# Attention and trigonometric FFN on one core: square roots as jobs of pairs of tiles, with new orders

## The chip, the cores and the metric

The kernel runs on 1 core of one Trainium2 chip. The time is device microseconds of one execution, as the median of several runs. The engines are TensorE (PE; PEld is its weight load), VectorE (DVE), ScalarE (ACT), GpSimd (POOL) and SyncE (SP), which issues nearly all DMAs.

## The reference, cut to what matters

`x` is (2, 2048, 512) float32, 4096 rows of 512. Context `ctx` is (2, 77, 512) with a mask over the 77 keys.

```python
def xattn(q, kv, mask):          # hid = 512, one head
    Q, K, V = q @ Wq + bq, kv @ Wk + bk, kv @ Wv + bv
    s = where(mask, einsum('bqh,bkh->bqk', Q, K) / sqrt(512), -1e9)
    return softmax(s) @ V @ Wo + bo

def ffn(x):
    real = x @ cos(theta + theta_noise)
    imag = x @ sin(phi + phi_noise)
    return sqrt(real * real + imag * imag)

x = x + xattn(layernorm(x), ctx, mask)
x = x + ffn(layernorm(x))
```

## The kernel before, in words

The rows are 32 tiles of 128 (t = 0 to 31). Two tiles are a pair (k2 = t // 2, 16 of them; one load of 512 KB each), four tiles a block (k = t // 4, 8 of them; softmax goes by block). First the weights are prepared: `Wq` and `Wk` are folded with the context into a 77-column matrix (scores), `Wv` and `Wo` into `VO`, and cos and sin of theta and phi into f16 weights, high part `WH` and low part `WL`.

Each tile then passes through: layernorm (statistics L612 to L630, normalised `xna` L638 or L640), split into an f16 high part (L643) and low part (L647), a transpose by DMA (L651, `xTa`), scores on TensorE (L694, L697, `s`), row maximum (L705), exp (L714, `e`), split of the probabilities into f16 parts in the buffer `E` (high L724 or L726, low L730 and L731; job names `eh`, `el`), a transpose of a whole block's `E` by DMA (L755, `et`, one for each block, `et7` the last), the product with `VO` (L794, L798, `o`; o28 is the one of tile 28), division and residual (L803), the second layernorm (`mw` L809, `xnb` or `xq` L861 on VectorE, L863 on ScalarE; the sum of squares L844 on ScalarE or L839 to L841 on VectorE; `vr` L849, L850), again a split (L643, L647 or, for the fast pairs, L872 to L884) and a transpose (`xTb` L651, `xU` L890; the job is `Tb`).

Then the FFN. Ordinary tiles take two groups of products into `f` (L945; f12 is that of tile 12) and square it on ScalarE (L998). Pairs 9 to 14 are "fast": both tiles share products of combined operands (L916, banks `f0`, `f1`, `fb`), a copy out of a bank (L926) and additions of banks on VectorE (L930, "combines") before the square (L933). Last, for every tile: the sum of the two squares (`ma`, L1004, into `mg`), the square root with the second layernorm's scale (`rt`, L1008, on ScalarE, table "sqrt"), the addition to `x` (`ou`, L1012) and the store (`st`, L1015). `ma` and `ou` may be on VectorE or POOL. Two tiles share a buffer `mg`. Tile 31 goes in three parts of 256, 128 and 128 columns.

None of this is in program order. Every step is an entry of `Jobs` with its engine, its assumed duration, the jobs it depends on, and the buffers it takes and releases. `Jobs.order()` is a planner: it goes through the jobs by a due time that stands for each job in the table `KEY`, charges `TABLE` = 1.28 us where a ScalarE job needs another table (`tab`), and writes out one order for every engine's queue, SP's included. The table `ENGINE` says for which jobs the second choice of engine is taken. The kernel is then issued in that order; on the chip each engine takes its queue strictly in order.

In the kernel before, the roots are one job for a block, which asks for four sums `ma` and both `vr`:

```python
add(("rt", k), "ACT", 2.58, [("ma", u, 0) for u in g] + [("vr", u // 2) for u in g if u % 2], lambda g=g: roots(g), tab="sqrt")
for u in g:
    add(("ou", u, 0), "POOL", 1.3, [("rt", k)], ...)
    add(("st", u, 0), "SP", 0.45, [("ou", u, 0)], ...)
```

The last block has a root for each tile, and for each part of tile 31.

Of the kernel before, what the change touches and what calls it, by code (L numbers as in the profile page):

```python
# [18 lines left out]
D = 512  # L19
# [16 lines left out]
ENGINE = {('VT', 1): 'DVE', ('wqT', 2): 'DVE', ('wqT', 3): 'DVE', ('tr', 1, 0, 2): 'DVE', ('tr', 1, 0, 3): 'POOL', ('tr', 1, 1, 2): 'DVE', ('tr', 1, 1, 3): 'POOL', ('xna', 0): 'DVE', ('loa', 4): 'POOL', ('loa', 5): 'POOL', ('loa', 6): 'POOL', ('loa', 7): 'POOL', ('loa', 8): 'POOL', ('loa', 9): 'POOL', ('hia', 10): 'DVE', ('loa', 10): 'POOL', ('nm1', 5): 'POOL', ('hia', 11): 'DVE', ('loa', 11): 'POOL', ('hia', 12): 'DVE', ('nm1', 6): 'POOL', ('loa', 13): 'POOL', ('loa', 14): 'POOL', ('xna', 17): 'DVE', ('loa', 21): 'POOL', ('xna', 23): 'DVE', ('hia', 23): 'DVE', ('loa', 25): 'POOL', ('xna', 26): 'DVE', ('hia', 26): 'DVE', ('loa', 26): 'POOL', ('loa', 27): 'POOL', ('xna', 30): 'DVE', ('loa', 30): 'POOL', ('loa', 31): 'POOL', ('et', 0, 1): 'ACT', ('et', 0, 2): 'ACT', ('eh', 3, 0): 'ACT', ('eh', 6, 0): 'ACT', ('eh', 7, 0): 'ACT', ('xnb', 0): 'ACT', ('xnb', 1): 'ACT', ('hib', 3): 'DVE', ('s2', 2): 'POOL', ('hib', 4): 'DVE', ('lob', 4): 'POOL', ('xnb', 5): 'ACT', ('hib', 5): 'DVE', ('xnb', 6): 'ACT', ('xnb', 7): 'ACT', ('hib', 7): 'DVE', ('lob', 8): 'POOL', ('xnb', 9): 'ACT', ('lob', 9): 'POOL', ('s2', 5): 'POOL', ('xnb', 10): 'ACT', ('lob', 10): 'POOL', ('bn2', 11): 'DVE', ('lob', 11): 'POOL', ('xnb', 12): 'ACT', ('hib', 12): 'DVE', ('lob', 13): 'POOL', ('s2', 7): 'POOL', ('xnb', 14): 'ACT', ('s2', 8): 'POOL', ('xnb', 16): 'ACT', ('hib', 16): 'DVE', ('xnb', 17): 'ACT', ('hib', 18): 'DVE', ('lob', 19, 1): 'POOL', ('s2', 10): 'POOL', ('xnb', 20): 'ACT', ('xnb', 21): 'ACT', ('qs', 20, 0): 'POOL', ('qs', 20, 2): 'POOL', ('lob', 21, 0): 'POOL', ('xnb', 22): 'ACT', ('xnb', 23): 'ACT', ('qs', 22, 1): 'POOL', ('qs', 22, 2): 'POOL', ('lob', 22, 0): 'POOL', ('lob', 22, 1): 'POOL', ('lob', 23, 0): 'POOL', ('xnb', 24): 'ACT', ('xnb', 25): 'ACT', ('qs', 24, 2): 'POOL', ('lob', 25, 0): 'POOL', ('lob', 25, 1): 'POOL', ('s2', 13): 'POOL', ('xnb', 26): 'ACT', ('xnb', 27): 'ACT', ('qs', 26, 1): 'POOL', ('qs', 26, 2): 'POOL', ('hib', 26): 'DVE', ('lob', 26, 0): 'POOL', ('lob', 26, 1): 'POOL', ('lob', 27, 0): 'POOL', ('lob', 27, 1): 'POOL', ('xnb', 28): 'ACT', ('xnb', 29): 'ACT', ('qs', 28, 0): 'POOL', ('hib', 28): 'DVE', ('hib', 29): 'DVE', ('lob', 29, 1): 'POOL', ('s2', 15): 'POOL', ('xnb', 30): 'ACT', ('lob', 30): 'POOL', ('xnb', 31): 'ACT', ('lob', 31): 'POOL', ('ma', 0, 0): 'DVE', ('ma', 3, 0): 'DVE', ('ou', 0, 0): 'DVE', ('ma', 4, 0): 'DVE', ('ma', 5, 0): 'DVE', ('ma', 7, 0): 'DVE', ('ou', 4, 0): 'DVE', ('ou', 5, 0): 'DVE', ('ou', 6, 0): 'DVE', ('ou', 7, 0): 'DVE', ('ma', 8, 0): 'DVE', ('ma', 9, 0): 'DVE', ('ou', 9, 0): 'DVE', ('ou', 10, 0): 'DVE', ('ma', 12, 0): 'DVE', ('ma', 15, 0): 'DVE', ('ou', 13, 0): 'DVE', ('ma', 16, 0): 'DVE', ('ma', 17, 0): 'DVE', ('ma', 18, 0): 'DVE', ('ou', 16, 0): 'DVE', ('ou', 17, 0): 'DVE', ('ou', 18, 0): 'DVE', ('ou', 23, 0): 'DVE', ('ma', 26, 0): 'DVE', ('ou', 24, 0): 'DVE', ('ou', 25, 0): 'DVE', ('ou', 26, 0): 'DVE', ('ou', 27, 0): 'DVE', ('ma', 28, 0): 'DVE', ('ma', 29, 0): 'DVE', ('ma', 30, 0): 'DVE', ('ma', 31, 0): 'DVE', ('ma', 31, 384): 'DVE'}  # L36
# [4 lines left out]
class Jobs:  # L41
# [11 lines left out]
    def add(self, name, eng, dur, deps, fn, alloc=(), rel=(), tab=None, size=0.0, alts=(), after=None, bank=None, lag=0.0, port=False, lead=0.87, alone=None):  # L53
        assert name not in self.jobs, name
        opts = [(eng, dur, port)] + [(a[0], a[1], len(a) > 3 and a[3]) for a in alts]
        for a in alts:
            if ENGINE.get(name) == a[0]:
                eng, dur, fn, port = a[0], a[1], a[2], len(a) > 3 and a[3]
        self.jobs[name] = dict(
            eng=eng, dur=dur, deps=list(deps), fn=fn, alloc=[t if isinstance(t, tuple) else (t, name) for t in alloc], rel=rel, tab=tab,  # L60
            size=size, opts=opts, after=after, bank=bank, lag=lag, port=port, lead=lead, alone=1.55 * size if alone is None else alone,
        )
# [117 lines left out]
def xattn_trig_ffn(  # L180
# [20 lines left out]
    V, A, G, T, S = nc.vector, nc.scalar, nc.gpsimd, nc.tensor, nc.sync  # L201
# [4 lines left out]
    NBLK = NT // 4  # L206
# [4 lines left out]
    wk = ctx.enter_context(tc.tile_pool(name="work", bufs=2))  # L211
# [7 lines left out]
    add = jobs.add  # L219
# [16 lines left out]
    warm = cst("warm", [P, 512], F16)  # L236
# [9 lines left out]
    R = cst("R", [P, 2, NB, D], F16)  # L246
# [6 lines left out]
    cg = cst("cg", [P, NB * NK])  # L253
    cgd = cst("cgd", [P, NB * NK])
    gs = cst("gs", [P, 1])
    bcol = cst("bcol", [P, 4, NC])
    brow = cst("brow", [16, P])
    msk = cst("msk", [P, NB, NK], mask.dtype)
    keep = cst("keep", [P, NB * NK])
    kscale = cst("kscale", [P, NB * NK])  # L260
    kneg = cst("kneg", [P, NB * NK])
    cxT = cst("cxT", [P, NC, NB * NK])
    VT = cst("VT", [P, NC, NB * NK])
    KT = cst("KT", [P, NC, NB * NK])
# [90 lines left out]
    for hc in range(NC):  # L355
# [5 lines left out]
            alts=(("DVE", 0.29, lambda hc=hc: V.tensor_scalar(VT[:, hc], D_["vt", hc], bcol[:, 2, hc : hc + 1], None, ALU.add)),))  # L361
# [41 lines left out]
    ssm, e2m, scm = bound("m", 1, ["mks"], P)  # L403
    ssv, _, scv = bound("v", NB, [f"vos{b}" for b in range(NB)], P, False)
    sce = cst("sce", [P, 1])
# [53 lines left out]
    for b in range(NB):  # L459
# [3 lines left out]
            alts=(("DVE", 0.6, lambda b=b: vo_ev(b, V.tensor_copy)),))  # L463
        sumsq(f"vos{b}", lambda b=b: vot(b), ssv[:, b : b + 1], 0.42, [("vb", b)])
        add(("vh", b), "ACT", 0.62, [("voe", b), "scv"], lambda b=b: vo_h(b, A),
            alts=(("DVE", 0.34, lambda b=b: vo_h(b, V), True),))
# [17 lines left out]
    for dc in range(NC):  # L484
# [4 lines left out]
            alts=(("DVE", 0.6, lambda ev=ev: ev(V.tensor_copy)),))  # L489
        add(("mk", dc), "PE", 1.05, [("wqT", dc)] + KTs + ([("mk", dc - 1)] if dc else []), lambda dc=dc: mk_mm(dc),  # L490
            alloc=("f",) if dc % 2 == 0 else (), rel=(("wqTh", dc // 2),))
    for h in range(2):
        def ev(E, h=h):
# [5 lines left out]
            alts=(("DVE", 0.45, lambda ev=ev: ev(V.tensor_copy)),))  # L499
# [4 lines left out]
        alts=(("DVE", 0.4, lambda: V.tensor_scalar(Mk[:, :, 0], D_["M"], scm, None, ALU.mult), True),))  # L504
# [93 lines left out]
    for i, a, b, op in SUMS if FAST else ():  # L598
        add(("ts", i), "DVE", 1.13, [quarter[a], quarter[b]] + before[i], lambda i=i, a=a, b=b, op=op: tsum(i, a, b, op, V), port=True,
            rel=(a, b), alts=(("POOL", 2.3, lambda i=i, a=a, b=b, op=op: tsum(i, a, b, op, G), True),))  # L600
# [67 lines left out]
    for t in range(NT):  # L668
        k = t // 2
# [7 lines left out]
        if t < 4 * DIRECT:  # L677
            add(("pa", t), "PE", 0.44, [("xna", t)], lambda t=t: turn("a", t), alloc=("m",), rel=(("xna", t),))
            add(("Ta", t), "ACT", 0.48, [("pa", t)], lambda t=t: keep_t(t, A.copy), alloc=("xTa",), rel=(("pa", t),),
                alts=(("DVE", 0.6, lambda t=t: keep_t(t, V.tensor_copy)),))  # L680
# [3 lines left out]
            alts=(("POOL", 1.17, lambda t=t: lo("a", t, G), True),))  # L684
# [321 lines left out]
    def root(t, w):  # L1006
        m = D_["mg", t // 2][:, t % 2, w[0] : w[1]]
        A.activation(m, m, AF.Sqrt, scale=VR[t // 2][:, t % 2 : t % 2 + 1])  # L1008

    def outp(t, E, w):  # L1010
        xo = xb[t][:, w[0] : w[1]]
        E.tensor_tensor(xo, xo, D_["mg", t // 2][:, t % 2, w[0] : w[1]], ALU.add)  # L1012

    def store(t, w):
        S.dma_start(of[t][:, w[0] : w[1]], xb[t][:, w[0] : w[1]])  # L1015

    for t in range(NT):
        k = t // 4
# [51 lines left out]
        if t % 4 == 3 and not last:  # L1070
            def roots(g):
                for t in g:
                    root(t, (0, D))
            g = range(t - 3, t + 1)
            add(("rt", k), "ACT", 2.58, [("ma", u, 0) for u in g] + [("vr", u // 2) for u in g if u % 2], lambda g=g: roots(g), tab="sqrt")
            for u in g:
                add(("ou", u, 0), "POOL", 1.3, [("rt", k)], lambda u=u: outp(u, G, (0, D)), rel=(("ma", u - u % 2, 0),),
                    alts=(("DVE", 0.6, lambda u=u: outp(u, V, (0, D)), True),), port=True)
                add(("st", u, 0), "SP", 0.45, [("ou", u, 0)], lambda u=u: store(u, (0, D)), rel=(("x", u // 2),), size=0.73, alone=0.87)
        elif k == NBLK - 1:  # L1080
            for w in parts:
                f = (w[1] - w[0]) / D
                q = (t, w[0])
                add(("rt",) + q, "ACT", 0.27 + 0.45 * f, [("ma",) + q, ("vr", t // 2)], lambda t=t, w=w: root(t, w), tab="sqrt")
                add(("ou",) + q, en, (0.6 if E is V else 1.3) * f, [("rt",) + q], lambda t=t, E=E, w=w: outp(t, E, w), port=True, rel=(("ma", t - t % 2, 0),))
                add(("st",) + q, "SP", 0.45, [("ou",) + q], lambda t=t, w=w: store(t, w), rel=(("x", t // 2),), size=0.73 * f, alone=0.87 * f)
# [37 lines left out]
```

## Time and profile before

| | us |
|---|---|
| median of 3 runs (lowest, highest) | 236.86 (236.34, 236.89) |
| the profiled execution: time | 237.07 |
| its span | 235.2 |
| PE, PEld busy | 225.7, 124.8 |
| DVE, ACT, POOL busy | 206.7, 193.7, 116.4 |

The mean granted clock of TensorE is 0.998. Busy time is the sum of an engine's instructions in the span; time and span differ by 1.87 us of start and end that the trace does not cover. All positions in the text are microseconds from the start of the span. `<-` in a row separates what an instruction writes from what it reads, or, behind an idle time, names what ended it.

### The profile page before, as it was taken

The page shows a single profiled execution, that of the slowest core. Times are in us where ns is not written, and L with a number is a line of the kernel's source. Part 1 is how long each engine was busy: PE and PEld are TensorE (multiplying, and loading weights), DVE is VectorE, ACT ScalarE, POOL GpSimd, SP SyncE. Part 2 cuts the span into 40 slices and gives each one's busy share as a digit, 9 for nine tenths or more (in the row PEclk, how much of TensorE's full clock was granted, in tenths as well). Part 3 has the DMA queues.
Part 4 walks back from the last instruction along what each step waited for, and adds up shares of the span by engine and source line. Part 5 has one row for each costly group of instructions (what it writes and reads, how often), then busy time and mean ns, then how long its engine had stood idle before and what let it go on. Part 6 is the DMA issues. An engine that isn't in the chain of part 4 may idle for free. (4 is left out here: it accounts for less than half of the span.)

```text
span 235.2 us, 4452 instructions
## 1 busy us (share of the span) xinstructions
PE 225.7 (96%) x1438; PEld 124.8 (53%) x1438; DVE 206.7 (88%) x592; ACT 193.7 (82%) x372; POOL 116.4 (49%) x116
## 2 busy tenths in 40 slices
PE   7999899999999999999999999999999898999992
PEld 2698797655445454444454456444444443444472
DVE  1779998899999999877977989999999979998972
ACT  2077999999999998997789499997879993897853
POOL 5116493931570706521762670631983589277340
PEclk9999999999999999999999999999999999999999
DMA  3999999955879799299879998998495746485543
GB/s 106 385 387 386 387 277 227 342 115 102 166 94 184 194 193 245 49 258 252 139 136 249 221 197 135 188 307 155 92 156 117 197 117 121 80 164 171 145 169 134
DMA packets 92725, 45.51 MB, mean 193 GB/s; under 512 B 79681, under 2 KB 80389, under 8 KB 92703
## 3 DMA queue, kind: packets, MB, share of 16 engines
q1 hardware_dynamic: 92431, 45.21, 81.6%
q8 instruction: 11, 0.18, 0.3%
q14 instruction: 11, 0.09, 0.1%
q10 hardware_dynamic: 144, 0.02, 0.0%
q0 software_dynamic: 128, 0.01, 0.0%
HBM read 17.12 MB, written 8.39 MB: 108 GB/s over the span
## 5 line engine op out<-in xcount | busy, mean ns | idle before, releaser
L945 PE MATMUL f<-WH,xTb 128*128 128x512 f16 (+2 forms) x352 | 87.0, 360 | 0.0
L945 PEld LDWEIGHTS <-xTb 128*128 128x128 f16 x528 | 49.1, 98 | 52.5 <-DMA xTb<-xsb 0.5
L945 PE MATMUL f<-WL,xTb 128*128 128x512 f16 (+2 forms) x176 | 50.2, 360 | 0.0
L916 PEld LDWEIGHTS <-xU 128*128 128x128 f16 x252 | 24.5, 98 | 30.5 <-issue 1.9
L1012 POOL TENSOR_TENSOR x<-x,mg 128x512 f32<-128x512 f32 x14 | 19.9, 1430 | 25.0 <-ACT mg L1008 24.9
L647 POOL TENSOR_TENSOR xsa<-xna,xsa 128x512 f16<-128x512 f32 x16 | 20.5, 1288 | 19.5 <-ACT xsa L643 14.2
L803 DVE SCALAR_TENSOR_TENSOR x<-o,ri,x 128x512 f32<-128x512 f32 x32 | 23.4, 745 | 4.1 <-PE o L798 3.4
L998 ACT ACTIVATE sq<-f 128x1024 f32<-128x1024 f32 (+2 forms) x22 | 20.7, 941 | 7.6 <-PE f L945 7.3
L640 ACT ACTIVATE xna<-x,nm,r 128x512 f32<-128x512 f32 x27 | 21.3, 807 | 4.8 <-DVE nm L630 4.5
L1004 POOL TENSOR_TENSOR mg<-sq 128x512 f32<-128x512 f32 x15 | 19.8, 1323 | 10.2 <-ACT sq L998 9.3
L916 PE MATMUL f<-tw,xU 128*128 128x512 f16 x108 | 24.6, 379 | 0.1
L612 DVE BATCH_NORM_STATS2 st<-x 128x6 f32<-128x512 f32 x32 | 21.0, 679 | 1.7 <-DMA x<-in_x_dram 1.7
L1008 ACT ACTIVATE mg<-mg,vr 128x512 f32<-128x512 f32 (+2 forms) x34 | 21.3, 687 | 1.1 <-DVE mg L1004 1.1
L623 POOL TENSOR_TENSOR r<-r,half 128x2 f32<-128x2 f32 x16 | 12.6, 791 | 14.7 <-DVE r L620 14.2
L647 POOL TENSOR_TENSOR xsb<-xnb,xsb 128x512 f16<-128x512 f32 x8 | 11.0, 1376 | 15.8 <-ACT xsb L643 14.7
L1004 DVE TENSOR_TENSOR mg<-sq 128x512 f32<-128x512 f32 (+2 forms) x19 | 15.8, 832 | 3.1 <-ACT sq L998 2.5
L884 POOL TENSOR_TENSOR xg<-xq,xg 128x512 f16<-128x512 f32 (+1 forms) x12 | 13.5, 1138 | 8.1 <-DVE xg L880 4.5
L930 DVE TENSOR_TENSOR sq<-f,sq 128x512 f32<-128x512 f32 x24 | 15.9, 678 | 1.7 <-PE f L916 1.7
L1012 DVE TENSOR_TENSOR x<-x,mg 128x512 f32<-128x512 f32 (+2 forms) x20 | 16.0, 824 | 1.4 <-ACT mg L1008 1.3
L933 ACT ACTIVATE sq<-sq 128x1024 f32<-128x1024 f32 x12 | 12.4, 1054 | 5.4 <-DVE sq L930 5.4
L697 PEld LDWEIGHTS <-xTa 128*128 128x128 f16 x336 | 14.2, 98 | 4.1 <-issue 0.3
L916 PE MATMUL fb<-WH,xU 128*128 128x512 f16 x48 | 15.9, 379 | 0.0
(174 smaller groups left out, 454.6 us busy)
## 6 DMA issues: line engine op xcount, KB each, us to landing
x<-in_x_dram SPq DMA_DIRECT2D x16, 512.0 KB, 7.4
out_dram<-x SPq DMA_DIRECT2D x31, 256.0 KB, 2.1
wk<-in_L_xattn_Wk_dram SPq DMA_DIRECT2D x4, 256.0 KB, 8.1
wq<-in_L_xattn_Wq_dram SPq DMA_DIRECT2D x4, 256.0 KB, 7.8
ph<-in_L_ffn_phi_dram SPq DMA_DIRECT2D x2, 512.0 KB, 6.5
phn<-in_L_ffn_phi_noise_dram SPq DMA_DIRECT2D x2, 512.0 KB, 5.8
th<-in_L_ffn_theta_dram SPq DMA_DIRECT2D x2, 512.0 KB
thn<-n_L_ffn_theta_noise_dram SPq DMA_DIRECT2D x2, 512.0 KB
```

The source lines that it names most:

```text
L612: V.bn_stats(st, xb[t])
L640: A.activation(xn, xb[t], AF.Identity, bias=nm[:, j : j + 1], scale=r[:, j : j + 1])
L647: E.tensor_tensor(xs[:, 1], D_["xn" + g, t], xs[:, 0], ALU.subtract)
L697: T.matmul(SPS[k][:, j, :NK], D_["xTa", t][:, s, c], Mk[:, c, m, ks], start=(n == 0), stop=(n == 3 * NC - 1))
L803: V.scalar_tensor_tensor(xb[t], AO[t], ri, xb[t], ALU.mult, ALU.add, accum_out=mv[:, 0:1])
L916: T.matmul(ps, xT[:, s, 2 * q + c], W, start=(c == 0 and n == 0), stop=(c == 1 and n == 2))
L930: V.tensor_tensor(sq_of(t + b[0])[:, b[1]], fbank(t, i), sq_of(t + a[0])[:, a[1]], ALU.add)
L945: T.matmul(FP[t, W0][:, h], D_["xTb", t][:, s, c], W[:, c, h, W0:W1], start=(c == 0 and s == 0 and W is WH and (h == 0 or not one)), stop= ...
L998: A.activation(D_["sq", t][:, :, w[0] : w[1]], FP[t, w[0]], AF.Square, scale=1.0 / SW)
L1004: E.tensor_tensor(D_["mg", t // 2][:, t % 2, w[0] : w[1]], sq[:, 0, w[0] : w[1]], sq[:, 1, w[0] : w[1]], ALU.add)
L1008: A.activation(m, m, AF.Sqrt, scale=VR[t // 2][:, t % 2 : t % 2 + 1])
L1012: E.tensor_tensor(xo, xo, D_["mg", t // 2][:, t % 2, w[0] : w[1]], ALU.add)
```

## The change

The roots become jobs of one pair of tiles (two sums, one `vr`, two roots), each followed by two `ou` and two `st`, for all blocks but the last, which stays as it was. Which pairs come behind one table load is no longer fixed by a job but by the order of the jobs. The tables `ENGINE` and `KEY` are made anew: about 90 jobs have another engine, and nearly all due times differ. Nothing else is changed: the same matmuls, buffers and shapes.

```diff
-ENGINE = {('VT', 1): 'DVE', ...
-KEY = {('warm', 0): 0.9959, ...
+ENGINE = {('VT', 1): 'DVE', ...
+KEY = {('warm', 0): 1.0, ...
...
-        if t % 4 == 3 and not last:
-            def roots(g):
-                for t in g:
-                    root(t, (0, D))
-            g = range(t - 3, t + 1)
-            add(("rt", k), "ACT", 2.58, [("ma", u, 0) for u in g] + [("vr", u // 2) for u in g if u % 2], lambda g=g: roots(g), tab="sqrt")
-            for u in g:
-                add(("ou", u, 0), "POOL", 1.3, [("rt", k)], lambda u=u: outp(u, G, (0, D)), rel=(("ma", u - u % 2, 0),),
-                    alts=(("DVE", 0.6, lambda u=u: outp(u, V, (0, D)), True),), port=True)
-                add(("st", u, 0), "SP", 0.45, [("ou", u, 0)], lambda u=u: store(u, (0, D)), rel=(("x", u // 2),), size=0.73, alone=0.87)
-        elif k == NBLK - 1:
+        if k < NBLK - 1:
+            if t % 2:
+                add(("rt", k2), "ACT", 1.29, [("ma", t - 1, 0), ("ma", t, 0), ("vr", k2)], lambda t=t: [root(u, (0, D)) for u in (t - 1, t)], tab="sqrt")
+                for u in (t - 1, t):
+                    add(("ou", u, 0), "POOL", 1.3, [("rt", k2)], lambda u=u: outp(u, G, (0, D)), rel=(("ma", u - u % 2, 0),),
+                        alts=(("DVE", 0.6, lambda u=u: outp(u, V, (0, D)), True),), port=True)
+                    add(("st", u, 0), "SP", 0.45, [("ou", u, 0)], lambda u=u: store(u, (0, D)), rel=(("x", u // 2),), size=0.73, alone=0.87)
+        else:
             for w in parts:
```

## The prediction

> **What bounds the kernel now.** I read the busy times first, then TensorE's waits, then the busy times by stretch, then the chain that ended last, and last the rows of the instructions that the change moves.
>
> The busy times, first line of the page's first part:
>
> ```profile
> PE 225.7 (96%) x1438; PEld 124.8 (53%) x1438; DVE 206.7 (88%) x592; ACT 193.7 (82%) x372; POOL 116.4 (49%) x116
> ```
>
> TensorE (PE) has 9.5 us free of a span of 235.2. Its work does not change here, so the time can fall only by what is idle on it, and rise by what is added to that. Where the idle time lies, from TensorE's waits (engine, line, releaser: us, times, longest):
>
> ```profile
> PE o L798 <- DMA et<-E: 0.7, 1, 0.7
> PE fb L916 <- DVE sq L930: 0.7, 1, 0.7
> PE o L794 <- ACT VO L438: 0.5, 1, 0.5
> ...
> PE o L798 <- DVE sq L930: 0.2, 1, 0.2
> ```
>
> The rest is head (1.2 us before the first matmul, about 1.3 in four small waits up to 29 us) and tail (4.3 us after the last matmul). The timeline puts the wait on `et` at 198.45 us, the two on `sq` at 185.68 and 199.74: 0.69 + 0.74 + 0.25 = 1.68 us in the stretch where block 7's softmax is due. Nothing stops TensorE from 46 to 185.
>
> Busy time by stretch (stretch, length, then PE, PEld, DVE, ACT, POOL, granted clock, DMA share, GB/s):
>
> ```profile
> 40.00:60.00 20.00, 19.46 (x165) 11.02 (x166) 19.29 (x61) 19.35 (x37) 8.68 (x8) 1.00 0.71 175
> 60.00:80.00 20.00, 19.94 (x123) 9.51 (x122) 19.78 (x61) 19.30 (x46) 10.36 (x10) 1.00 0.90 159
> ...
> 100.00:120.00 20.00, 20.00 (x94) 9.10 (x93) 16.96 (x60) 16.36 (x30) 7.87 (x9) 1.00 0.95 213
> 120.00:140.00 20.00, 20.00 (x165) 10.70 (x163) 16.47 (x58) 16.13 (x34) 11.67 (x11) 1.00 0.93 203
> 140.00:160.00 20.00, 20.00 (x144) 10.24 (x143) 19.41 (x56) 19.74 (x48) 6.63 (x7) 1.00 1.09 209
> 160.00:180.00 20.00, 20.00 (x103) 9.23 (x102) 19.36 (x49) 16.82 (x27) 12.34 (x13) 1.00 0.76 133
> 180.00:200.00 20.00, 18.26 (x103) 8.35 (x102) 18.12 (x42) 15.27 (x31) 15.43 (x14) 1.00 0.59 136
> ```
>
> VectorE (DVE) is second: 97 to 98% busy from 40 to 80 and from 140 to 180, with one stretch of slack, 100 to 140 (6.6 us idle). It is also VectorE that ends the late waits. The chain that ended last begins on it:
>
> ```profile
> 195.00 1.79 DVE sq L930 x3
> ...
> 199.74 0.59 PE o L798 x2
> ...
> 220.39 10.49 PE f L945 x96
> ```
>
> so before 200 us VectorE's order sets the end, after it TensorE's.
>
> **The roots.** All instructions at the root's line:
>
> ```profile
> L1008 ACT ACTIVATE mg<-mg,vr x34: 401/707/723, 75.7 to 231.6; 128x512 f32<-128x512 f32 x31, 128x128 f32<-128x128 f32 x2, 128x256 f32<-128x256 f32 x1
> L1008 ACT ACT_TABLE_LOAD  x5: 1283/1283/1283, 74.4 to 203.4; - x5
> ```
>
> Roots stay 34, of the same shapes. Of table loads the written orders have 14 in each kernel: 5 for the root, 6 for exp, 3 others. Pairs 0, 1, 2 share a load, then 3 to 5, 6 alone, 7 to 9, and 10 to the end; exp of blocks 5 and 6 now shares one. So the root edit by itself costs ScalarE 0.00 us. A rule speaks against it: the Trainium skill, "ScalarE: Activation LUTs", section "What ACT_TABLE_LOAD costs", puts a switch at 1283 ns plus a drain of about 1380, and its section "Rules for kernel authors" wants one set finished before switching. Here the quad's load at 203.37 begins 0.01 us after the ScalarE work before it ended, and its first root 0.01 us after the load: 1.28, and no drain of 1.38 is to be seen. With an extra return to the roots (two loads) ScalarE would pay 2.57 us by this row; by the page it would be 5.3. The orders have no such return, so neither enters the sum.
>
> What pairs do change is when sums of squares `mg` are used up and when `ou` and `st` can go. In the profile ahead of `ou`, POOL's idle of 24.9 us is put down to the root (7 times). POOL is busy for 49%, nobody waits for it there, and a gain on it is worth nothing. Stores now stand in pairs in SP's queue, some ahead of transposes (out x6 ahead of `et5`, x10 and x11 ahead of block 14's `xU`), so a late root pair holds SP and the transposes behind it. Just before `et7` the queue was idle in the trace (last issue ahead of it 189.68, `et7` 195.06), so I price that at 0; its bound is one root pair with out-adds, 2 x 0.71 + 2 x 0.68 = 2.8 us.
>
> **Work that changes engine.** The choice of engine is made anew for about 90 jobs. By the two written orders, priced with the trace's rows (start to next start; means, which include waits for the port):
>
> ```profile
> L1004 DVE TENSOR_TENSOR mg<-sq x19: 292/683/1941, 59.7 to 231.3; 128x512 f32<-128x512 f32 x16, 128x128 f32<-128x128 f32 x2, 128x256 f32<-128x256 f32 x1
> L1004 POOL TENSOR_TENSOR mg<-sq x15: 1266/1275/1715, 60.2 to 217.1; 128x512 f32<-128x512 f32 x15
> ```
>
> - VectorE gains: L1004 five more x 0.87 = 4.33; L647 four x 0.61 = 2.45; L926 two (ScalarE before) x 0.70 = 1.40, no such row on VectorE, the nearest being L930 at 0.68; L643 two, 0.70; L861, L874 and the statistics L839-L841, 1.66 together; L724 two (the `eh` of blocks 6 and 7, ScalarE before), 0.51.
> - VectorE loses: L1012 two, 1.66; L880 four, 1.76; L630 seven, 0.87; L638 0.65; L884 0.60; others 0.56.
> - Sum: +11.05 - 6.10, unrounded +4.93 us for VectorE. POOL -4.75, ScalarE +0.26.
>
> At medians instead of means (0.68 for L1004, of which a part is waiting for POOL's port) it would be about +4.0; with less on POOL the waits shrink too. I keep 4.93.
>
> **Where it lands.** Adding the rows down VectorE's queue, the extra stands at about 0 where 60 us were reached, at +5 at the last step before `Tb12` (used by TensorE at 118.58, landed 115.58: 3.0 us of slack), +5.4 at the copy of `E` ahead of `et7`, +7.5 at block 14's last combine, and +4.93 at the end. TensorE's uses move by -2.6 to +2 us. So VectorE must run fuller by about 5 us, and nearly all of that must come out of 100 to 140.
>
> *Block 7's softmax.* In the trace its last scores end at 183.69, the copy of `E` at 195.00, `et7` lands at about 198.4 (3.4 later), and TensorE, there at 197.71, starts at 198.45. In the new order 12 more matmuls of 0.216 stand ahead of the last scores (+2.6: 186.3 without waits) and 42 instead of 60 behind them (9.1 us in place of 13.0), so TensorE is at its first use of `et7` at 195.4, with 1.3 us more of its queue left than before. The end is where it was if that use starts at 198.45 + 0.25 - 1.30 = 197.4; no wait at all is worth 1.68.
>
> When `et7` lands depends on VectorE: 179.2 us of its rows stand up to the copy of `E`. It idled 10.7 us up to 60 (20 - busy of the stretches), mostly for the first loads, which stay. With x us idle from 60 on, the copy ends at 179.2 + 10.7 + x = 189.9 + x and `et7` lands at 193.3 + x. In the trace x was about 9.6 (20.3 idle up to the copy). At the 97% that VectorE reaches in its fullest stretches, x = 0.03 x 130 = 3.9 and `et7` lands at 197.2, 0.2 before the point of no change.
>
> *Block 14.* From that copy to block 14's last combine VectorE has 26.3 us of rows where it had 24.2, +2.1; TensorE from its first use of `et7` to f30, whose banks come behind those combines, has 22.5 for 21.2, +1.3. VectorE falls behind by another 0.8.
>
> *Head and middle.* `VO` is taken from its bank earlier on ScalarE, which may cut the 0.54 at 43.73; f12 and f16 have their transposes +5 to +6 later on VectorE against slacks of 2 to 3 us, and may wait 0.5 to 0.8. Such a wait gives VectorE time and is given back at `et7`, so I enter neither. The tail (parts of tile 31, their roots, out-adds and stores, 4.3 us) has the same order in both: 0.
>
> **Sum.** Profiled run before 237.07 (span 235.2, 1.87 around it; 0.21 above the median 236.86): + 0.00 roots - 0.2 `et7` + 0.8 block 14 = 237.7. A measurement of this kernel tells about 0.3% (0.7 us) from no change; this is just beyond it.
>
> **Rivals.**
> - *Faster: the slack of 100 to 140 takes all the added work.* It was idle because producers came late there (2.46 us for `o` at 107, 1.56 for `e` at 129), and pairs give VectorE sums and out-adds to do meanwhile. It decides if x stays under 2.5: `et7` lands before 195.8, no late wait is left, 237.07 - 1.68 = 235.4. For it: 6.6 us idle lie just there. Against it: 98% over 130 us, which VectorE keeps in one stretch only.
> - *No change:* x near 3.5, the late waits gone at `et7` and back at block 14: 236.9.
> - *Much slower: VectorE paces from 100 on.* At 95%, x = 6.5 and `et7` lands at 199.8: + 2.4 + 0.8 = 240.3.
> - *The edit does nothing by itself:* the same 14 loads, 34 roots, equal work on TensorE; the time is that of the new order alone. The orders show this already; it is part of all cases above.
>
> **How the numbers follow.** Forecast and the slower rival together 0.48 (0.33 up to 239, 0.15 beyond), no change 0.24, faster 0.28. Range 235.4 (no late wait) to 240.2 (VectorE at 95%); about 1 in 10 lies on either side: below, if the 0.54 at 43.73 goes as well; above, if SP holds transposes too.
>
> **What would show it.** Right: 14 table loads; DVE busy near 211.6, POOL near 111.6; DVE at 95% or more from 100 to 140; TensorE's longest waits at `et7` (`o` L798) and on `sq` L930 behind 190 us, 1.7 to 3 us in all. The faster case: no wait of TensorE over 0.3 us behind 60 us. Wrong in kind: more than 14 loads; a long wait of TensorE before 150 us; waits on transposes held up behind a store in SP's queue; or a tail unlike 4.3 us.

## The result, and the profile after

| | before | after |
|---|---|---|
| median, us (lowest to highest) | 236.60 (235.35 to 236.89, 4 runs) | 239.59 (238.76 to 240.51, 4 runs) |
| ratio, 95% interval | 1 | 1.0149 (1.0107 to 1.0191) |
| the profiled execution: time, span | 237.07, 235.2 | 239.72, 237.9 |

The changed kernel is slower by 3.0 us in the medians and by 2.65 us between the two profiled executions (239.72 - 237.07), on which the rest of this section rests. The recorded ratio is not the quotient of the two medians (1.013), which lies in its interval. The busy times of the profile after:

```profile
PE 226.0 (95%) x1438; PEld 125.0 (53%) x1438; DVE 208.6 (88%) x595; ACT 194.7 (82%) x369; POOL 109.9 (46%) x118
```

TensorE does the same work in the same time (226.0 for 225.7); what is added is idle time on it, 11.9 us for 9.5. VectorE has 1.9 us more and POOL 6.5 less. TensorE's waits say which engine ended the idle time:

```profile
PE f L916 <- DVE sq L930: 1.7, 1, 1.7
PE o L798 <- DMA et<-E: 1.5, 2, 1.0
...
PE o L798 <- DVE nb L705: 0.5, 1, 0.5
PE o L798 <- DVE x L803: 0.4, 1, 0.4
```

and its timeline where the larger ones lie (start, length; the idle time and what ended it stand in brackets):

```profile
66.42 0.59 PE L798 MATMUL o<-R,et 128*128 128x512 f16 x2 [0.55 <-DVE nb L705]
67.39 0.59 PE L798 MATMUL o<-R,et 128*128 128x512 f16 x2 [0.39 <-DVE x L803]
74.54 1.48 PE L798 MATMUL o<-R,et 128*128 128x512 f16 x6 [0.52 <-DMA et<-E]
...
196.49 1.46 PE L916 MATMUL f<-tw,xU 128*128 128x512 f16 x6 [1.73 <-DVE sq L930]
200.21 1.04 PE L798 MATMUL o<-R,et 128*128 128x512 f16 x4 [0.97 <-DMA et<-E]
```

So the loss lies in two places. From 64 to 76 us, in the softmax of blocks 1 and 2, TensorE now stands for 0.55 + 0.39 + 0.52 = 1.46 us; before, nothing stopped it there. From 184 to 205 us, around block 7's softmax, it stands for 2.7 us where it stood for 1.68. Together that is +2.5 us; the rest of the span, the tail included (4.4 for 4.3 us), is equal within 0.3. In between VectorE is fuller than before, but far from full where its slack was (stretch, length, then PE, PEld, DVE, ACT, POOL):

```profile
100.00:120.00 20.00, 20.00 (x114) 9.52 (x113) 18.05 (x63) 18.34 (x38) 8.34 (x9) 1.00 0.90 207
120.00:140.00 20.00, 20.00 (x154) 10.48 (x153) 18.33 (x63) 18.87 (x41) 9.46 (x11) 1.00 0.96 202
...
180.00:200.00 20.00, 17.43 (x120) 8.47 (x117) 17.48 (x40) 14.36 (x26) 14.73 (x13) 1.00 0.59 107
```

91% from 100 to 140, and TensorE is never idle there. The roots are as the orders had them, 34 with a median of 712 ns, and five loads:

```profile
L1008 ACT ACT_TABLE_LOAD  x5: 1283/1283/1283, 68.1 to 192.3; - x5
```

The row that I had not looked at is the last copy into `E`, which `et` waits for (counts, shortest/median/longest ns). First the kernel before, then after:

```profile
L731 DVE COPY E<-E x7: 233/237/1191, 59.5 to 193.8; 128x308 f16<-128x308 f16 x7
```

```profile
L731 DVE COPY E<-E x7: 237/1194/1314, 59.3 to 194.1; 128x308 f16<-128x308 f16 x7
```

The same seven copies: one long before, four long after, at 59.27, 70.08, 155.12 and 194.06 us. VectorE's and POOL's timelines at the second of them, after:

```profile
69.35 0.42 DVE L643 CAST xsb<-xnb 128x512 f16<-128x512 f32 x1
69.69 0.47 DVE L730 SCALAR_TENSOR_TENSOR E<-e,E 128x308 f16<-128x308 f32 x1
70.08 1.20 DVE L731 COPY E<-E 128x308 f16<-128x308 f16 x1
```

```profile
69.85 1.33 POOL L647 TENSOR_TENSOR xsb<-xnb,xsb 128x512 f16<-128x512 f32 x1 [1.52 <-DVE xsb L643]
```

VectorE's own cast (L643, the high part of a later tile, placed right ahead of the split of `E`) releases the low part on POOL; the copy then ends 0.10 us after POOL's instruction does (71.28 after 71.18). At the three other places it ends 0.10 us after POOL's running L647 (at 59 us), L1012 (155) and L884 (194). The three other copies take 0.24 us.

### The profile page after: what moved, and what is told of

It is laid out like the page before. It is cut to its first block, busy times and chain, and to the rows that moved or that the text cites. A ratio compares the mean times of both kernels' runs of the same rounds, so it can differ in the third digit from the quotient of the medians.

```text
span 237.9 us, 4454 instructions
## 1 busy us (share of the span) xinstructions
PE 226.0 (95%) x1438; PEld 125.0 (53%) x1438; DVE 208.6 (88%) x595; ACT 194.7 (82%) x369; POOL 109.9 (46%) x118
## 4 chain that ended last, share of the span: by engine, by line
PE 63%; DMA 18%; ACT 9%; DVE 6%; issue 1%; SPq 1%; DVEq 0%; ACTq 0%
PE f L945 35%; PE f L916 13%; PE fb L916 8%; DMA x<-in_x_dram 5%; PE o L798 5%; DMA wq<-in_L_xattn_Wq_dram 3%; DMA et<-E 3%; DMA wk<-in_L_xattn_Wk_dram 3%; DMA xTa<-xsa 3%; PE s L697 3%; ACT xna L640 1%; DVE st L612 1%; DVE E L731 1%; ACT sq L998 1%; ACT WH L555 1%
## 5 line engine op out<-in xcount | busy, mean ns | idle before, releaser
L1012 POOL TENSOR_TENSOR x<-x,mg 128x512 f32<-128x512 f32 x16 | 21.7, 1367 | 20.3 <-ACT mg L1008 20.3
L640 ACT ACTIVATE xna<-x,nm,r 128x512 f32<-128x512 f32 x28 | 22.3, 805 | 6.1 <-POOL nm L630 5.5
L916 PE MATMUL f<-tw,xU 128*128 128x512 f16 x108 | 25.6, 379 | 1.8 <-DVE sq L930 1.7
L623 POOL TENSOR_TENSOR r<-r,half 128x2 f32<-128x2 f32 x16 | 14.6, 912 | 26.8 <-DVE r L620 19.4
L647 POOL TENSOR_TENSOR xsa<-xna,xsa 128x512 f16<-128x512 f32 x13 | 16.0, 1241 | 20.1 <-DVE xsa L643 11.0
L1008 ACT ACTIVATE mg<-mg,vr 128x512 f32<-128x512 f32 (+2 forms) x34 | 22.2, 690 | 1.4 <-POOL mg L1004 0.7
L1004 POOL TENSOR_TENSOR mg<-sq 128x512 f32<-128x512 f32 x10 | 14.1, 1416 | 12.6 <-ACT sq L933 6.4
L884 POOL TENSOR_TENSOR xg<-xq,xg 128x512 f16<-128x512 f32 (+1 forms) x13 | 14.4, 1124 | 10.8 <-ACT xg L880 10.2
L930 DVE TENSOR_TENSOR sq<-f,sq 128x512 f32<-128x512 f32 x24 | 16.1, 683 | 3.7 <-PE f L916 3.3
L1004 DVE TENSOR_TENSOR mg<-sq 128x512 f32<-128x512 f32 (+2 forms) x24 | 15.3, 636 | 3.0 <-ACT sq L998 3.0
L798 PE MATMUL o<-R,et 128*128 128x512 f16 (+1 forms) x56 | 15.3, 380 | 2.4 <-DMA et<-E 1.5
L697 PE MATMUL s<-Mk,xTa 128*128 128x77 f16 x336 | 15.1, 199 | 0.0
```

What stands on the lines that cost most here:

```text
L640: A.activation(xn, xb[t], AF.Identity, bias=nm[:, j : j + 1], scale=r[:, j : j + 1])
L697: T.matmul(SPS[k][:, j, :NK], D_["xTa", t][:, s, c], Mk[:, c, m, ks], start=(n == 0), stop=(n == 3 * NC - 1))
L798: T.matmul(ops, ET[k][:kc, j, h], R[:kc, h, k // BPB], start=(h == 0), stop=(h == 1))
L916: T.matmul(ps, xT[:, s, 2 * q + c], W, start=(c == 0 and n == 0), stop=(c == 1 and n == 2))
L930: V.tensor_tensor(sq_of(t + b[0])[:, b[1]], fbank(t, i), sq_of(t + a[0])[:, a[1]], ALU.add)
L1004: E.tensor_tensor(D_["mg", t // 2][:, t % 2, w[0] : w[1]], sq[:, 0, w[0] : w[1]], sq[:, 1, w[0] : w[1]], ALU.add)
```

## The experiments

Two theories stood against each other. *The cost sits in places of the order:* few jobs on VectorE stand badly, at the softmax of blocks 1, 2 and 7, and moving them gives the time back. *VectorE is too full*, as my prediction had it: moving jobs only moves the waits. A third question was what the pairs by themselves do.

All kernels but the two at the end keep the planner's order of the one or the other kernel and move single jobs in it, each ahead of another job; the engine of each job stays, unless said:

```diff
-    for n in jobs.order():
+    todo = jobs.order()
+    for n, m in MOVES:
+        todo.remove(n)
+        todo.insert(todo.index(m), n)
+    for n in todo:
```

Ratios are to the kernel before, with 95% intervals; the changed kernel is at 1.0149. Line numbers above 1070 aside, all kernels have the same, but for the one with ten buffers, whose lines come one later.

**Block 7's split earlier.**

```diff
+MOVES = [(('eh', 7, 0), ('cp', 24)), (('el', 7, 0), ('cp', 24))]
```

> After's order, with one move on VectorE: the split of block 7's probabilities (eh7, el7) goes ahead of the copy of bank f0 of pair 12 (cp24), that is from behind cp24 and two combines that wait for products to right behind qs 26. Theory (the cost sits in places of the order, here at et7): E's copy is done near 191.3 instead of 195.25, et7 lands before TensorE asks for it, the waits of 1.73 us (f on a combine) and 0.97 us (o on et) go, L730 and L731 run before POOL's lo parts of pair 13 begin and take 0.5 and 0.24 us: 2.0 to 2.7 us less than the changed kernel, about 237.0. Rival (VectorE is simply too full): the wait comes back behind 200 us, 239.1 to 239.6.

Measured: 237.83 us, 1.0083 (1.0055 to 1.0112). About 0.66% or 1.6 us comes back, less than the 2.0 to 2.7 of the theory and far more than the rival's 0.5. The copy of `E` ends at 191.3 us, the wait on `et7` is gone, and that on the combine is halved:

```profile
192.54 1.45 PE L916 MATMUL f<-tw,xU 128*128 128x512 f16 x6 [0.87 <-DVE sq L930]
```

What stays is the place of the combine (o4 of pair 11) behind the copy cp24.

One thing in this trace was not moved. The copy of `E` in block 2, with the same instructions ahead of it as in the changed kernel, where it took 1.20 us, is short here:

```profile
70.44 0.24 DVE L731 COPY E<-E 128x308 f16<-128x308 f16 x1
```

The wait on `et2` is gone with it. The profiled execution is the fastest of the six (237.23), so part of what it gained may come from there and not from the move.

**The splits of blocks 1 and 2 ahead of the casts.**

```diff
+MOVES = [(('el', 1, 0), ('hia', 12)), (('el', 2, 0), ('hib', 4))]
```

> After's order, with two swaps on VectorE: el1 goes ahead of the cast hia12, el2 ahead of the cast hib4; these casts release lo parts on POOL, which in the trace ran just when E's copy (L731) wanted to. Theory: L731 takes 0.24 us in place of 1.2 at both, and TensorE's waits between 64 and 76 us (0.55 + 0.39 + 0.52) go; of the 1.46 us some is lost again at block 7, where et7 is bound by VectorE: 238.2 to 239.1. Rival (VectorE too full): L731 shorter, but within 0.3 of the changed kernel's 239.6.

Measured: 238.84 us, 1.0118 (1.0092 to 1.0143), about 0.7 us less; by the times alone that is not settled, since the intervals of this kernel and of the changed one overlap. The first two long copies take 0.24 us, those at 155 and 194 stay long. The wait on `et2` is gone; the two before it are not:

```profile
67.08 0.59 PE L798 MATMUL o<-R,et 128*128 128x512 f16 x2 [0.43 <-DVE nb L705]
68.07 0.59 PE L798 MATMUL o<-R,et 128*128 128x512 f16 x2 [0.40 <-DVE x L803]
```

There I was wrong: those banks are late because statistics of tile 16 stand ahead of the maxima and residuals that free them, not because of the copy at 59 us (the tuned kernel below moves these statistics, and both waits go).

**Both.** `MOVES` holds the four moves of both kernels.

> After's order with the moves of both other kernels (eh7, el7 ahead of cp24; el1 ahead of hia12; el2 ahead of hib4). Theory (cost in places): all five waits gone, 239.6 - 2.7 - 1.4 = 235.5, at most 236.5. Rival (VectorE too full): 239 or more.

Measured: 236.58 us, 1.0030 (1.0012 to 1.0048). The gains add up: of the 1.5% that the change had cost, 1.2% come back, 0.3% are left, with the same engines for all jobs, the same matmuls and the same pairs. That rules out the rival as the main cause: VectorE was not too full. Its busy time is 206.2 us here, 2.4 less than in the changed kernel, so that at least this much of its busy time there was waiting.

**Tuned further.** Two more moves: `('oc', 22, 'o4')` ahead of `('cp', 24)`, and the statistics `('bn1', 16)` behind the residual of tile 5.

> The changed kernel with the moves of both (1.003) and two more: the combine of pair 11 (o4) ahead of the copy cp24, which frees the bank that TensorE waited 0.87 us for, and the statistics of tile 16 behind the residuals of tiles 4 and 5, which free the banks it waited 0.43 and 0.39 us for. Theory (cost in places): 0.6 to 1.5 us less, ratio 0.997 to 1.001. Rival (VectorE too full): 1.003.

Measured: 235.83 us, 0.9970 (0.9939 to 1.0001). The waits on banks fell to 0.28 us and to nothing; a wait of 0.70 us on `et2` came back, whose transpose stands behind tile 14's in SP's queue. In the last kernel I moved that as well (`bn1` 16 behind `el2`, tile 14's transpose behind `et2`, its scores behind the products with `et2`):

> The last tuned form of the changed kernel (0.997) with its wait of 0.70 us on et2 taken up: the statistics of tile 16 behind el2 (0.6 us earlier copy of E), et2 ahead of tile 14's transpose in SP's queue, and the scores of tile 14 behind the three products that use et2. Theory (cost in places): that wait goes, 0.3 to 0.7 us less than the last, ratio 0.993 to 0.996. Rival (something else is late next, tile 14's scores or block 7 again): 0.997 to 0.999.

Measured: 236.27 us, 0.9989 (0.9967 to 1.0011), no gain over the last. The wait on `et2` is gone, and TensorE waits 0.64 us for the next transpose instead:

```profile
75.36 0.60 PE L945 MATMUL f<-WH,xTb 128*128 128x512 f16 x2 [0.64 <-DMA xTb<-xsb]
```

Here the rival's description fits: the wait moved on by one transfer.

**The same repair in the kernel before.** There the split of block 7 was held too (1.21 and 1.19 us).

```diff
+MOVES = [(('eh', 7, 0), ('hib', 26)), (('el', 7, 0), ('hib', 26))]   # and eh7 on VectorE
```

> The kernel before, with the split of block 7's probabilities moved: eh7 from ScalarE to VectorE, and eh7, el7 ahead of the cast hib26 that lets POOL start the lo parts of pair 13. Before, L730 and L731 took 1.21 and 1.19 us there. Theory (POOL's lo parts hold E's split): they take about 0.47 and 0.24, et7 lands about 3 us earlier, TensorE's waits of 0.74 and 0.25 us go, 0.5 to 1.0 us faster than before (ratio 0.996 to 0.998); the wait of 0.69 on a combine at 185.7 stays. Rival (products' banks bind there): ratio 1.000.

Measured: 235.47 us, 0.9981 (0.9954 to 1.0008). All seven copies now take 0.23 to 0.24 us, `et7` is issued at 190.62 instead of 195.06 us, and no wait on it is left; but a wait of 1.08 us on the combine behind it (f, L930, at 192.4) took the place of the three. With `eh7`, `el7` behind those combines and the cast hib26 behind them:

> The kernel before with VectorE's order at block 7 once more changed: eh7 (on VectorE) and el7 behind the two combines of pair 11 that free the bank for f1 of pair 12, and the cast hib26 behind them (in the last one hib26 stood ahead of the combines and TensorE waited 1.08 us for the bank). Theory: neither et7 nor the bank is late, all of the 1.68 us of late waits go, ratio to before 0.992 to 0.996. Rival (something else is late next, pair 13's transposes, since its lo parts start 1 to 2 us later): 0.997 to 1.002.

Measured: 235.53 us, 0.9968 (0.9930 to 1.0007). The wait on `et7` stays away; 0.69 us on a combine at 185.3 is still there, which was to go as well, and two of 0.33 and 0.27 us in pair 14's products (210 and 213 us) are new. The two tuned kernels, 0.9968 from before and 0.9970 from after, are the lowest of this study; the interval of neither excludes 1, so that either beats the kernel before is not settled.

**The pairs by themselves.** The roots of some blocks are put back to four at a time, in the changed kernel's order.

```diff
+MOVES = [(('rt', 0), ('rt', 1)), (('ou', 0, 0), ('nm2', 10)), (('st', 0, 0), ('nm2', 10)),
...
+         (('x', 9), ('nm2', 10)), (('rt', 2), ('rt', 3)),
...
```

> After's order, with the roots of blocks 0, 1 and 5 again done four at a time: the first pair's roots, out-adds and stores are put back to those of the second pair (the load of x pair 9, which needs a buffer of block 0, goes behind its stores). The price of pairs by themselves. Theory (pairs cost nothing, the new order does): 239.6, within 0.7. Rival (the pairs' out-adds on POOL and stores on SP come at bad moments): 238.5 or less. Against both: if the early stores and loads that pairs allow are worth something, 240.3 or more.

Measured: 245.84 us, 1.0396 (1.0351 to 1.0440). Part of that is my placing: out-adds on VectorE stood right behind the roots in the order, and VectorE waited for them:

```profile
DVE x L1012 <- ACT mg L1008: 7.5, 5, 2.3
```

> The quad kernel again, for blocks 0 and 1 alone, with the out-adds of the first pair placed right ahead of those of the second (in the last one they stood right behind the roots in the queues, and VectorE waited 7.5 us for them). The loads of x pairs 9 and 11, which need those blocks' buffers, go behind their stores. If the 6 us of the quad kernel were my placing: within 0.7 of the changed kernel, ratio 1.012 to 1.018. If pairs really buy something in this order (earlier out-adds, stores and loads of x): ratio 1.02 or more. If pairs cost: 1.011 or less.

Measured: 243.42 us, 1.0328 (1.0286 to 1.0369). Those waits fell to 1.8 us, and another is on top of VectorE's list:

```profile
DVE st L612 <- DMA x<-in_x_dram: 5.2, 5, 2.9
```

The first statistics of later tiles wait for the loads of x, which need the buffers of pairs whose stores are now late; TensorE then waits 1.47 us for `et3` (at 113.6) and 0.90 for a transpose behind it.

```diff
+    BUFS = BUFS | dict(x=10)      # nine before; the loads of x 9 and 11 keep their places
```

> The quad kernel of blocks 0 and 1 again (roots and out-adds placed as in the second one), but the loads of x pairs 9 and 11 stay where the changed kernel has them, and x gets ten buffers in place of nine, so that no load needs a buffer of a pair whose store is now late. If what the pairs buy in this order is that x's buffers come free a pair at a time: close to the changed kernel, ratio 1.010 to 1.020, and VectorE's waits on loads of x (5.2 us in the second quad kernel) are gone. If it is something else (the buffers of mg, the stores in SP's queue): 1.028 or more, as in the second quad kernel.

Measured: 239.51 us, 1.0115 (1.0065 to 1.0165). VectorE's wait on loads of x is down to 1.2 us.

So in this order the pairs of blocks 0 and 1 alone are worth about 1.8% (1.0328 against 1.0149), and what they are worth is x's buffers coming free two tiles at a time: with one more buffer, and the loads at their old places, the roots may wait for four tiles without loss. The changed kernel with ten buffers was not run.

**Order and engines apart.** One kernel has the changed kernel's order and the engines of before, the other the reverse (`add` plans with one table `ENGINE`, the jobs are issued by the other).

> The changed kernel's order of jobs, but every job on the engine it had before (VectorE loses what it was given, POOL gets it back). If the time is lost because VectorE has more to do: faster than the changed kernel, ratio to before 1.000 to 1.008. If it is lost in places of the order: no gain, 1.015 or more, since the order was planned for other engines.

> The order of jobs of before, every job on the engine of the changed kernel. If VectorE's work is the cost: ratio about 1.01 to 1.015, the same loss as the changed kernel. If the order and its engines only work together: 1.02 or more. If neither matters: 1.00.

Measured: 249.72 us, 1.0585 (1.0545 to 1.0624), and 257.30 us, 1.0904 (1.0858 to 1.0950). Both lose far more than the change, with VectorE busy for 218.5 and 220.7 us: an order fits only the engines it was planned for. On whether the 1.9 us of VectorE's work cost anything they say nothing.

## Why the prediction was right, and where it was not

The direction and the range (235.4 to 240.2) held, the 239.6 near the upper end, beside the rival in which VectorE paces (240.3). That nearness does not bear the rival out: moves that left VectorE all its jobs gave back four fifths of the loss. The size did not hold: +0.6 us was worked out, +2.65 came. That the range held is in part luck, since terms that were too big (VectorE's work by 3.0 us, block 14 by 0.8) stood against others that were missing (1.5 us at blocks 1 and 2, 1.5 on the transpose `et7`). Term by term:

- *Roots, 0.00.* Right: 14 table loads, 34 roots of the same length.
- *The edit does nothing by itself.* Wrong, and it was said to be shown by the orders. I followed `rt` to `ou` and `st` and stopped there; the store also frees a buffer of x, and the loads of later pairs hang on it. The quad kernels show that this is what the new order uses.
- *VectorE +4.93 us.* Measured +1.9. The term of L1004 failed: five more x 0.87 = 4.33 by means of before. Its 24 instructions together took 15.3 us, less than the 19 before (15.8). Five of those 19 took 0.80 to 1.94 us, each while an instruction of POOL ran, together 3.9 us more than at the median; of the 24 none is that long. Whether that is because POOL has less to do, or because its instructions now stand elsewhere, was not separated.

```profile
L1004 DVE TENSOR_TENSOR mg<-sq x24: 292/682/696, 64.5 to 233.9; 128x512 f32<-128x512 f32 x21, 128x128 f32<-128x128 f32 x2, 128x256 f32<-128x256 f32 x1
```

 Against that, L731, for which I entered nothing since its count is the same, went from 2.6 to 5.6 us. A mean that holds waits for another engine is not a price: the wait goes with its partner in time, not with the instruction.
- *Block 7, -0.2.* Measured +1.0 (1.73 + 0.97 against 1.68). I had `et7` from how full VectorE is, with the copy of `E` at 193.8; it ended at 195.25. In the terms of that sum, VectorE's instructions up to the copy took 176.6 us and not 179.2, and it idled 7.4 us from 60 us on and not 3.9: emptier than I had it, and later all the same. (For the kernel before I had put that idle time at 9.6 us; the trace has 10.6, which does not enter the sum.) What made the copy late is not fullness but place: the split stood behind a copy and two combines that waited for products (0.47 us of waiting just ahead), and L730 and L731 took 1.31 and 1.19 us beside POOL's L884.

  The wait on `et7` itself has one more part. From the copy's end to TensorE's use I took 3.4 us; it was 5.0 (195.25 to 200.21). Four transposes are queued right behind `et7` in both kernels, so they do not explain it. In between, the DMAs all but stopped (last number of a row, GB/s; it is 194 from 198.0 to 199.5 in the kernel before):

```profile
198.50:199.00 0.50, 0.50 (x4) 0.13 (x2) 0.50 (x2) 0.00 (x0) 0.50 (x1) 1.00 1.42 11
199.00:199.50 0.50, 0.24 (x2) 0.00 (x0) 0.49 (x2) 0.00 (x0) 0.50 (x1) 1.00 0.06 6
```

 At 197.94 us, just ahead of that, the trace has a packet of 16 KB of the kind "instruction"; before, such a packet came at 193.36, ahead of `et7`. The kernel with block 7's split moved has one at 196.87 and 5 to 10 GB/s from 197.5 to 198.5, where no transpose was waited for. With the 3.4 us of before, `et7` would have landed at about 198.7 (an estimate from these rows), ahead of TensorE, which was there at 199.24. So the 0.97 us hang on those 1.5 us; that the packet is their cause was not tested.
- *Block 14, +0.8.* Did not come: from 200.21 us to the last matmul TensorE shows no wait of note.
- *Head and middle, 0.* f12 and f16, which I said might wait 0.5 to 0.8 us, did not wait. The wait of 0.54 at 43.73 went, and two of 0.28 and 0.40 us at 44 and 46 came. But the softmax of blocks 1 and 2, which I passed over, cost 1.46 us. In the trace of before `et2` landed at 72.60 and TensorE began its weights at 72.64. After, where TensorE did wait for it, the same 0.04 us lie between (74.49 and 74.53), so before there was no slack at all: a row that I should have put into the sum.
- *What would show it.* Right were the 14 loads and the places of the late waits (`et7` and a combine behind 190 us, 2.7 us in all). Wrong were VectorE at 95% from 100 to 140 (91%), DVE near 211.6 (208.6) and no long wait before 150.

With these terms the 0.6 us become 0.6 - 0.8 + 1.2 + 1.5 = 2.5 of the 2.65. So the loss was forecast with the right engine and, at block 7, in the right place, but with the wrong reason: sums of work along a queue. The moves show that the cause is in the main which instruction stands ahead of which; at `et2` it is also which of two engines came first in that execution (last section).

## What to carry to other kernels

When an order is made anew, look first at the few places where a wait ended within some tenths of a microsecond before, and list what now stands ahead of the producer there, on its engine and on the engine it shares a port with; totals of work say little, since four moved jobs gave back four fifths here of what the whole change had cost. A cast that starts another engine's work belongs behind, not ahead of, the last step before a critical transfer. And follow a buffer past its last reader to the next load: that is where smaller jobs paid off.

## What was not expected of the hardware

A short f16 copy on VectorE waits for the whole POOL instruction that got in ahead of it: 0.24 us alone, 1.19 to 1.32 us in each case where that was a POOL L647, L884 or L1012. Not every POOL instruction holds it: at 129.73 us, after, the copy ran inside POOL's L623 (128x2 values, 129.50 to 130.40) and took 0.24 us; why was not tested. The Trainium skill, "SBUF — State Buffer", section "SBUF: two separate sides", says that the shared port pair is an exclusive lock and that whoever starts first has it for the whole instruction; the traces agree on the lock for L647, L884 and L1012. They also show how little decides. In the kernel before, VectorE's and POOL's timelines at `el2` are, in relative times, those of the kernel after:

```profile
67.68 0.47 DVE L730 SCALAR_TENSOR_TENSOR E<-e,E 128x308 f16<-128x308 f32 x1
68.07 0.24 DVE L731 COPY E<-E 128x308 f16<-128x308 f16 x1
```

```profile
67.84 1.47 POOL L647 TENSOR_TENSOR xsb<-xnb,xsb 128x512 f16<-128x512 f32 x1 [1.05 <-DVE xsb L643]
```

POOL starts 0.16 us after L730 both times; before, the copy went first and POOL took 1.47 us, after, POOL went first (1.33 us) and the copy took 1.20. Three kernels of this study have the same instructions there as the kernel after, with POOL's start 0.23 us ahead of the copy's in all of them: with block 7's split moved the copy took 0.24 us, in the two quad kernels with nine buffers 1.20 and 1.19. So the order of the queues does not settle it, and the 0.52 us on `et2` of the changed kernel may be there in one execution and not in another. The cast placed behind the split takes the choice away: 0.24 us in the four kernels that have it. What decides otherwise was not tested.
